# A gate and up product of seven half products with running sums in PSUM, and the quantizer of h behind attention's sums, in a linear-attention layer gated by an FP4 feed-forward net

## Chip, cores and metric

One core of one Trainium2 chip runs one program. The engines are PE (TensorE, the matmuls), DVE (VectorE), ACT (ScalarE), POOL (GpSimd) and SP (SyncE, which here only issues DMAs). The metric is the device time of one execution in microseconds (us); lower is better. Everything is float32 unless a type is named.

## What is computed

For an input x of 4 x 2048 tokens by 256 features:

```python
xn = layernorm(x)
# attention and its own feed-forward net
Q, K = elu(xn @ Wq + bq) + 1, elu(xn @ Wk + bk) + 1      # 16 heads of 64
V    = xn @ Wv + bv
KV   = einsum("bshd,bshm->bhdm", K, V)                    # sums over all 2048 tokens of a batch
Z    = 1 / (einsum("bshd,bhd->bsh", Q, K.sum(axis=1)) + EPS)
o    = einsum("bshd,bhdm,bsh->bshm", Q, KV, Z)
x1   = layernorm(xn + o @ Wo + bo) * g1 + be1
s    = layernorm(x1 + gelu(x1 @ W1 + b1) @ W2 + b2) * g2 + be2
# the gate: a feed-forward net whose inputs and weights are rounded to FP4 in blocks of 16
h    = silu(fp4(xn) @ fp4(w_gate).T) * (fp4(xn) @ fp4(w_up).T)   # 704 wide
g    = silu(fp4(h) @ fp4(w_down).T)
out  = x + s * g
```

`fp4(t)` divides each block of 16 neighbours by the block's largest absolute value over 6, rounds to the eight magnitudes 0, 0.5, 1, 1.5, 2, 3, 4, 6, and multiplies the scale back in.

## The kernel before

The 8192 tokens are cut into 32 blocks of 256 tokens (T), eight to a batch; a block is two tiles of 128 tokens (j = 0, 1). KV needs all keys of a batch before its first query, so the keys of batch 0 are made in a start phase (lines 1055 to 1152), and the keys of batch b+1 are made beside the queries of batch b. A pass over keys handles one half (f) of the key features for one block of tokens, two such passes to each query block: f=0 for the first four blocks of a batch, f=1 for the other four. The f=0 keys are normalized from x in the stage ahead, stored, and transposed by DMA (`keys_apart`: ACT copies into a tile with the tag "e", which the e of Q uses too); the f=1 keys are loaded again. Blocks 24 to 31 have no keys beside them. The keys of a stage are made ready in the stage before.

The loop over n (line 1170 on) is a pipeline. Stage n finishes block n's quantized h and x in qT, makes `sums` of its queries (pz, then z = 1/pz on DVE, stored to DRAM as z_d and read back as zb, each row spread over 64 partitions), runs `gate_up(n+1)`, `down(n)`, multiplies Q by zb (`qz`), runs `attention(n)` with its normalization, the second half of the feed-forward net of block n-1 (py), its output, the queries of block n+1 (pq) and the first half of the feed-forward net of block n (pf). On PE each stage is therefore: pk, pz, pxk, pg, pd, pk, pa, pxk, py, pt_x, pscale, py, pq, pf.

What sets the order. `mm` (line 102) and `tr` (105) keep PE's instructions in program order. DVE and ACT go through the `Ordered` helper (111 to 122, so all their rows show L119): in program order in the start phase, and from line 1145 on in an order that the scheduler chooses ahead of time, within waits that `tc.issue_after` adds. Every DMA of the stages is issued from SP's queue, one after the other, and an issue that waits holds up those behind it. All matmuls share four PSUM banks of the tag "mm" and some accumulators.

Around the gate: `gate_up` (753) makes, for each token tile j and each half i of 352 columns, a gate product and an up product in one bank each, over two 128-deep chunks c of the features: 16 matmul calls. ACT takes silu of the one bank, DVE multiplies by the other. The weights are `wgu`, [128, chunk, gate columns then up columns], filled in `quantize_gu` from transpositions. After the third product pair the instruction named "late" ends; `qz` waits for it.

The quantizer of h has two parts: `scales_h` (701; a reduction of 704 columns, the scale, its reciprocal) and `grid_of_h` (704; h times reciprocal, ACT's `m_h`, rounding onto h, and the grid in bfloat16), for each j. The grid is transposed by DMA into gridT (738); the scales of h and x go through PE (`pscale`), ACT, a DRAM tile scale_d (726) and eight spreading DMAs (729) into qT, and `quantized_x` and `quantized_h` (742, 748) multiply the two.

Attention in the first three batches is a product by seven as well (`seven_sums`, `seven_products`, `add_seven`, lines 889 to 922): `attention_sums` makes four sums of halves of Q (zs) behind qz. `WEIGHT` (880) names which weight each of the seven products takes. `m_of_half` (608) turns the key sums pxk into the matrix of a half of the heads when its last keys are done; it reloads wv (616), copies pxk to xk, stores a row of it (631) and reads that back as kh (636).

Of the kernel before, what the change touches and what calls it, by code (L numbers as in the profile page):

```python
# [8 lines left out]
F32 = mybir.dt.float32  # L9
# [13 lines left out]
def linear_attention_gated_by_fp4_ffn(  # L23
# [228 lines left out]
    wv_sb, wv_d = {}, {}  # L252

    def load_wv(f, dep):
        wv_sb[f] = batch.tile([P, ND, HALF], F32, tag="wv", name=f"wv_{f}", bufs=1)
        load_when(dep, wv_sb[f], by_chunks(Wv)[:, :, f * HALF : (f + 1) * HALF])

    def wv_bias(f):
        bias_in_row0("v", wv_sb[f], f, nc.gpsimd)
        wv_d[f] = dram.tile([P, ND, HALF], F32, tag=f"wv_d{f}", name=f"wv_d{f}", bufs=1)  # L260
        nc.sync.dma_start(wv_d[f], wv_sb[f])
        if f > 0:
            del wv_sb[f]

    cols = {}

# [69 lines left out]
        return x.rearrange("p (k e) -> p k e", e=BLK)  # L336


    wgu = const.tile([P, ND, 2 * I], F32, name="wgu")
    wd = const.tile([P, NI, D], F32, name="wd")  # L340
    nc.gpsimd.memset(wd[TAIL:, NI - 1, :], 0.0)

# [28 lines left out]
    def quantize_gu(ks):  # L371


        w = work.tile([P, I], F32, tag="h", name=f"wgu_{ks[0]}")
        for i, k in enumerate(ks):
            lo, hi = k * P, (k + 1) * P
            cs = slice(i * D, (i + 1) * D)
            if hi <= I:
                nc.sync.dma_start(w[:, cs], w_gate[lo:hi, :])
            elif lo >= I:  # L380
                nc.sync.dma_start(w[:, cs], w_up[lo - I : hi - I, :])
            else:
                nc.sync.dma_start(w[: I - lo, cs], w_gate[lo:I, :])
                nc.sync.dma_start(w[I - lo :, cs], w_up[: hi - I, :])
        yield from quantize_weight(w, len(ks) * D, f"wgu_{ks[0]}")
        for i, k in enumerate(ks):
            pt = mm_tile(f"pwgu_{k}")
            for c in range(ND):
                lo = i * D + c * P
                tr(pt[:, c * P : (c + 1) * P], w[:, lo : lo + P], ident)  # L390
            scalar.copy(
                wgu[:, :, k * P : (k + 1) * P], pt[:, : ND * P].rearrange("p (c k) -> p c k", c=ND)
            )
        yield

    def load_down():
# [211 lines left out]
    def m_of_half(b, f, dep=None, ahead=False):  # L608


        nm = f"{b}_{f}"
        if wv_sb.get(f) is not None:
            wv = wv_sb.pop(f)
        else:
            wv = batch.tile([P, ND, HALF], F32, tag="wv", name=f"wv_{nm}", bufs=1)
            nc.sync.dma_start(wv, wv_d[f])
        wo = batch.tile([P, 4, D], F32, tag="wo", name=f"wo_{nm}", bufs=1)
        load_when(dep, wo, by_chunks(Wo)[:, 4 * f : 4 * f + 4, :])
        if ahead:
# [3 lines left out]
            nc.gpsimd.memset(kh[b], 0.0)  # L623
        m = m_sb[b, f] = batch.tile([P, 4, D], F32, tag=f"m{f}", name=f"m_{nm}", bufs=2 - f)
        pxk = keys.pop((b, "pxk", f))
        xk = batch.tile([P, ND, HALF], F32, tag="xk", name=f"xk_{nm}", bufs=1)
        for d in range(ND):
            scalar.copy(xk[:, d, :], pxk[d])

# [112 lines left out]
    def quantized_x(n):  # L742

        qx = qT[:, NI:, :]
        t = gridT[n][:, NI * TB :, :].rearrange("p (c j) t -> p c (j t)", j=TB)
        return vector.tensor_tensor(qx, qx, t, ALU.mult)

    def quantized_h(n, j):

# [1 line left out]
        return vector.tensor_tensor(qh, qh, gridT[n][:, j * NI : (j + 1) * NI, :], ALU.mult)  # L751

    def gate_up(n):
        blk[n]["h"] = []
        for j in range(TB):
            h = work.tile([P, I], F32, tag="h", name=f"h_{n}_{j}")
            blk[n]["h"].append(h)
            for i in range(2):
                halves = []
                for part in range(2):  # L760
                    pg = mm_tile(f"pg_{n}_{j}_{i}_{part}")[:, :IH]
                    lo = part * I + i * IH
                    for c in range(ND):
                        mm(
                            pg, qT[:, NI + c, j * P : (j + 1) * P], wgu[:, c, lo : lo + IH],
                            start=c == 0, stop=c == ND - 1,
                        )
                    halves.append(pg)
                    if part == 0:
                        yield  # L770
                hh = h[:, i * IH : (i + 1) * IH]
                scalar.activation(hh, halves[0], AF.Silu)
                ins = vector.tensor_tensor(hh, hh, halves[1], ALU.mult)
                if (j, i) == (1, 0):
                    blk[n]["late"] = ins.ins
                yield

    def down(n, j):
        if j == 0:
# [285 lines left out]
    for n in range(NB):  # L1065
# [50 lines left out]
        if n == 5:  # L1116
            add_b2(dep)
        if n == 6:
            load_xn(0)
            scales_x(0)  # L1120
            spread_scales(-1, False, True)
# [6 lines left out]
    load_xn(1)  # L1128
    load_xnT(0)

    step(gate, 4)
    step(ready)
    step(m_0)
    scales_h(0, 0)
    scales_x(1)
    step(gate, 4)
    scales_h(0, 1)
    step(m_0, 2)
    m_half = m_of_half(0, 1)
# [30 lines left out]
    for n in range(NBLK):  # L1170
# [78 lines left out]
            load_xn(n + 2)  # L1249
        if subs:  # L1250
            keys_xk(b + 1, subs[1])
            if subs[1] % NB == NB - 1:
                m_half = m_of_half(b + 1, subs[1] // NB)
                step(m_half)
        bn, bin_ = divmod(n + 1, NB)
        next_subs = (2 * bin_, 2 * bin_ + 1) if bn + 1 < B else ()
        for sub in next_subs if n > 0 else ():
# [2 lines left out]
            ffn_2(n - 1, 20)  # L1260
        more = n + 1 < NBLK, n + 2 < NBLK
        if more[0]:
            scales_h(n + 1, 0)
            behind = zs_ins if n == 0 else None if subs else qz_ins
            with tc.issue_after(behind) if behind is not None else nullcontext():
                scales_h(n + 1, 1)
            if more[1]:
                scales_x(n + 2)
        for sub in next_subs if n == 0 else ():
# [13 lines left out]
            spread_scales(n + 1, *more)  # L1283
        if n > 0:
            ffn_2(n - 1, 28)
        if more[0]:
            q_of(n + 1)
        if n == 0:
# [73 lines left out]
```

## Time and profile before

| what | value |
| --- | --- |
| median of 3 runs | 1878.16 us (1877.71 to 1878.72) |
| span of the profiled execution | 1880.7 us |
| one stage with keys (18, first pg to the next first pg) | 1248.93 - 1192.49 = 56.44 us |
| one stage of the last batch (28) | 1756.63 - 1712.49 = 44.14 us |
| first pg of the start phase | 127.91 us |

The profile is of one execution and its times stand against its own span. In a row of the groups the columns are line, engine, operation, out<-in with partitions x elements and type, count; then busy time, mean ns of one; then the engine's idle time just before such rows and what ended most of it. In a timeline a row is start, duration, engine, line, operation, tiles, count, and in brackets the idle time before it with what ended it. A matmul of float32 shows as two instructions. Durations of neighbours overlap a little, as the engines are pipelined, so steps are also taken from start to start.

### The profile page before, as it was taken

The numbers are of one execution on the slowest core, as the hardware profiler recorded it, in microseconds if no ns is written. First come the engines' busy times: TensorE is split into PE (matmuls) and PEld (weight loads), VectorE is DVE, ScalarE is ACT, GpSimd is POOL, SyncE is SP. The second block draws the span as 40 slices with busy tenths as digits, with TensorE's granted clock in tenths as the row PEclk, the third lists the DMA queues.
The fourth block names the chain that finished last, engine by engine and source line by source line (L and its number), as shares of the span: only waits on it lengthen the run. The fifth ranks groups of instructions, "written<-read, shape, count | busy, mean of one in ns | idle before, by whom it ended". The sixth has DMA issues, their size and how long they took to land.

```text
span 1880.7 us, 25219 instructions
## 1 busy us (share of the span) xinstructions
PE 1861.7 (99%) x9324; PEld 1383.0 (74%) x9324; DVE 1363.6 (73%) x2526; ACT 706.7 (38%) x1191; POOL 386.9 (21%) x371
## 2 busy tenths in 40 slices
PE   9999999999999999999999999999999999999998
PEld 4456677777777777777677787777777788888887
DVE  5676777766677877777667787776676767777775
ACT  2333544333334335443233533353322333333332
POOL 1411322011122212220112221122101122222212
PEclk9999999999999999999999999999999999999999
DMA  5526564434535456635344544564543544444442
GB/s 184 193 73 130 117 124 103 96 101 94 96 64 94 115 98 122 143 66 111 80 89 79 117 100 103 96 139 87 95 86 72 104 75 87 82 90 83 88 84 54
DMA packets 229434, 188.78 MB, mean 100 GB/s; under 512 B 107687, under 2 KB 191155, under 8 KB 229310
## 3 DMA queue, kind: packets, MB, share of 16 engines
q1 hardware_dynamic: 228476, 185.58, 47.4%
q8 instruction: 74, 1.21, 0.3%
q10 hardware_dynamic: 834, 1.58, 0.3%
q14 instruction: 50, 0.41, 0.1%
HBM read 131.96 MB, written 32.59 MB: 87 GB/s over the span
## 4 chain that ended last, share of the span: by engine, by line
PE 78%; DVE 11%; DMA 7%; issue 1%; POOL 1%; SPq 1%; ACT 1%; POOLq 0%; ACTq 0%; DVEq 0%
PE pg L103 13%; PE pf L103 11%; PE pk L103 10%; PE pxk L103 10%; PE pq L103 9%; PE pa L103 8%; PE pd L103 7%; PE py L103 7%; DMA zb<-z_d 3%; PE pz L103 2%; DMA z_d<-z 1%; DVE y L119 1%; DMA xn<-xn_d 1%; DVE x L119 1%; DVE hs L119 1%
## 5 line engine op out<-in xcount | busy, mean ns | idle before, releaser
L430 POOL TENSOR_TENSOR rstd<-rstd,neg_half 128x2 f32<-128x2 f32 (+1 forms) x98 | 77.8, 795 | 1298.0 <-DVE rstd L119 984.9
L103 PE MATMUL pg<-wgu,qT 128*128 128x352 f32 x1024 | 308.5, 459 | 0.1
L103 PEld LDWEIGHTS pg<-wgu,qT 128*128 128x128 f32 x1024 | 194.3, 190 | 113.7 <-issue 11.5
L103 PE MATMUL pk<-wk_sb,xnT_k 128*128 128x512 f32 x512 | 230.4, 592 | 1.2 <-ACT xnT_k L119 1.2
L103 PE MATMUL pq<-xnT,wq_sb 128*128 128x256 f32 x1024 | 227.6, 380 | 1.5 <-DVE zq L119 1.4
L103 PE MATMUL pxk<-kk,xn_k 128*128 128x512 f32 x496 | 227.9, 598 | 1.0 <-DVE kk L119 1.0
L103 PE MATMUL pf<-x1T,w_sb 128*128 128x256 f32 x1024 | 227.2, 380 | 1.1 <-DVE zq L119 0.6
L103 PEld LDWEIGHTS pf<-x1T,w_sb 128*128 128x128 f32 x1024 | 193.8, 190 | 30.4 <-DVE zq L119 4.0
L103 PEld LDWEIGHTS pq<-xnT,wq_sb 128*128 128x128 f32 x1024 | 191.8, 190 | 27.7 <-DVE zq L119 3.1
L119 DVE SCALAR_TENSOR_TENSOR kk<-ek,pk 128x512 f32<-128x512 f32 x128 | 85.6, 685 | 173.2 <-ACT ek L119 173.2
L103 PE MATMUL pd<-wd,qT 128*128 128x256 f32 x768 | 172.9, 380 | 0.0
L103 PEld LDWEIGHTS pk<-wk_sb,xnT_k 128*128 128x128 f32 x512 | 97.0, 190 | 102.6 <-issue 89.0
L119 ACT ACT_TABLE_LOAD x121 | 155.2, 1283 | 40.9 <-PE pk L103 26.0
L119 ACT ACTIVATE x1T<-pt_x,bcol 128x256 f32<-128x256 f32 x64 | 32.7, 561 | 359.3 <-PE pt_x L106 359.3
L103 PEld LDWEIGHTS pd<-wd,qT 128*128 128x128 f32 x768 | 145.3, 190 | 26.4 <-issue 2.5
L103 PEld LDWEIGHTS pxk<-kk,xn_k 128*128 128x128 f32 x496 | 89.4, 190 | 99.1 <-issue 87.3
L119 DVE TENSOR_TENSOR h<-h,pg 128x352 f32<-128x352 f32 x128 | 66.1, 517 | 107.1 <-PE pg L103 104.0
L119 ACT ACTIVATE h<-pg 128x352 f32<-128x352 f32 x128 | 58.9, 460 | 209.8 <-PE pg L103 209.7
L119 ACT ACTIVATE hT<-pf,bcol 128x256 f32<-128x256 f32 x256 | 106.1, 472 | 66.7 <-PE pf L103 66.3
L119 DVE TENSOR_TENSOR zq<-zq,zb 128x1024 f32<-128x1024 f32 x64 | 78.9, 1232 | 68.9 <-DMA zb<-z_d 68.8
L103 PE MATMUL py<-w_sb,hs 128*128 128x128 f32 x992 | 122.0, 275 | 0.0
L119 ACT ACTIVATE e<-pq,neg_one 128x512 f32<-128x512 f32 x128 | 86.2, 685 | 83.7 <-PE pq L103 71.2
(161 smaller groups left out, 2777.8 us busy)
## 6 DMA issues: line engine op xcount, KB each, us to landing
zb<-z_d SPq DMA_DIRECT2D x128, 256.0 KB, 6.2
qT<-scale_d SPq DMA_DIRECT2D x248, 128.0 KB, 6.0
x_k<-in_L_attn_src_dram SPq DMA_DIRECT2D x32, 256.0 KB, 4.1
x<-in_L_attn_src_dram SPq DMA_DIRECT2D x32, 256.0 KB, 2.9
xn_d<-xn_k SPq DMA_DIRECT2D x32, 256.0 KB, 2.5
xn<-xn_d SPq DMA_DIRECT2D x32, 256.0 KB, 2.7
xnT_d<-xnT_k SPq DMA_DIRECT2D x32, 256.0 KB, 2.0
xnT<-xnT_d SPq DMA_DIRECT2D x32, 256.0 KB, 4.3
```

The source lines that it names most:

```text
L103: return tc.keep_in_program_order(nc.tensor.matmul(*args, **kw))
L119: ins = op(*args, **kw)
L430: pool["last"] = nc.gpsimd.tensor_tensor(rstd[:, j0:j1], rstd[:, j0:j1], neg_half[:, j0:j1], ALU.pow).ins
```

## The change

Five edits go together.

1. `gate_up` splits the product into halves three ways: two token tiles, two feature chunks, and gate or up columns. Seven products of halves replace eight (the scheme that attention uses), each for two column halves u: 14 matmul calls. The weights are seven [128, 704] tiles, of which four are sums that POOL makes once, in the start phase. The left sides need four 128 x 128 sums of quantized x, which DVE makes behind `quantized_x`. The products are not summed by VectorE alone: a product is accumulated onto a bank that already holds others, after ACT or DVE has read the sum so far.
2. The quantizer's scales of h (both j) come behind the instruction `zs_ins`, or `qz_ins` in the last batch, in every stage.
3. To make room, wv and xk share a tile with the tag of zb, the first loads of wv use the tag of wo, and wv is reloaded from DRAM each time.
4. `m_of_half` of the loop starts behind the last part of `ffn_2(n - 1)`.
5. The end of the start phase is ordered anew: the weight of `down` first, then the gate, with the scales of h behind its parts.

```diff
+    wgu = const.tile([P, 7, I], F32, name="wgu")
+    def gate_sums():
+        nc.gpsimd.tensor_tensor(wg("t3"), wg("22"), wg("t1"), ALU.subtract)
+        nc.gpsimd.tensor_tensor(wg("t1"), wg("t1"), wg("11"), ALU.subtract)
+        nc.gpsimd.tensor_tensor(wg("t2"), wg("22"), wg("t1"), ALU.subtract)
+        nc.gpsimd.tensor_tensor(wg("t4"), wg("21"), wg("t2"), ALU.subtract)
...
+        t = work.tile([P, 2, ND, HALF], F32, tag="zb", name=f"wv_xk_{nm}", bufs=1)
+        wv, xk = t[:, 0], t[:, 1]
+        nc.sync.dma_start(wv, wv_d[f])
...
     def quantized_x(n):
-        return vector.tensor_tensor(qx, qx, t, ALU.mult)
+        vector.tensor_tensor(qx, qx, t, ALU.mult)
+        s = blk[n + 1]["xs"] = work.tile([P, 4, P], F32, tag="x1T", name=f"xs_{n + 1}", bufs=1)
+        h = quarters_of(qx)
+        vector.tensor_tensor(s[:, 0], h["21"], h["22"], ALU.add)
+        vector.tensor_tensor(s[:, 1], s[:, 0], h["11"], ALU.subtract)
+        ins = vector.tensor_tensor(s[:, 3], h["12"], s[:, 1], ALU.subtract)
+        vector.tensor_tensor(s[:, 2], h["11"], h["21"], ALU.subtract)
+        return ins
...
     def gate_up(n):
+        run = banks("pg")
+        product(1, run, True)
+        for u in range(2):
+            scalar.copy(h[0][:, part[u]], run[u])
+        yield
+        other = banks("pg5")
+        product(5, other, True)
+        for u in range(2):
+            scalar.copy(up[1][u], other[u])
+        yield
+        product(6, run, False)
+        for u in range(2):
+            scalar.copy(up[0][u], run[u])
+        yield
+        product(3, other, False)
+        for u in range(2):
+            vector.tensor_tensor(up[0][u], up[0][u], other[u], ALU.add)
+        yield
+        product(7, run, False)
+        for u in range(2):
+            vector.tensor_tensor(up[1][u], up[1][u], run[u], ALU.add)
+        yield
+        last_ = banks("pg2")
+        product(2, last_, True)
+        for u in range(2):
+            hh = h[0][:, part[u]]
+            vector.tensor_tensor(hh, hh, last_[u], ALU.add)
+            scalar.activation(hh, hh, AF.Silu)
+            blk[n]["late"] = vector.tensor_tensor(hh, hh, up[0][u], ALU.mult).ins
+        yield
+        product(4, run, False)
+        for u in range(2):
+            hh = h[1][:, part[u]]
+            scalar.activation(hh, run[u], AF.Silu)
+            vector.tensor_tensor(hh, hh, up[1][u], ALU.mult)
+        yield
...
+            gate_sums()
             load_xn(0)
...
+    step(ready)
     step(gate, 4)
-    step(ready)
     step(m_0)
+    scales_x(1)
+    step(gate, 2)
     scales_h(0, 0)
-    scales_x(1)
-    step(gate, 4)
+    step(gate, 1)
     scales_h(0, 1)
...
-            scales_h(n + 1, 0)
-            behind = zs_ins if n == 0 else None if subs else qz_ins
-            with tc.issue_after(behind) if behind is not None else nullcontext():
-                scales_h(n + 1, 1)
+            with tc.issue_after(zs_ins if in_seven(b) else qz_ins):
+                for j in range(TB):
+                    scales_h(n + 1, j)
...
             ffn_2(n - 1, 28)
+        if subs and subs[1] % NB == NB - 1:
+            m_half = m_of_half(b + 1, subs[1] // NB)
+            step(m_half)
```

`product(i, bank, start)` makes product i for both column halves; `start=False` accumulates onto what the bank holds.

## Prediction

> **What bounds the kernel now.** I read the page's engine totals and clock first, then the chain that ended last, then the groups by shape, and then timelines of one block of each kind.
>
> ```profile
> PE 1861.7 (99%) x9324; PEld 1383.0 (74%) x9324; DVE 1363.6 (73%) x2526; ACT 706.7 (38%) x1191; POOL 386.9 (21%) x371
> ...
> PEclk9999999999999999999999999999999999999999
> ...
> PE 78%; DVE 11%; DMA 7%; issue 1%; POOL 1%; SPq 1%; ACT 1%; POOLq 0%; ACTq 0%; DVEq 0%
> ...
> L103 PE MATMUL pg<-wgu,qT 128*128 128x352 f32 x1024 | 308.5, 459 | 0.1
> ...
> L119 DVE TENSOR_TENSOR zq<-zq,zb 128x1024 f32<-128x1024 f32 x64 | 78.9, 1232 | 68.9 <-DMA zb<-z_d 68.8
> ```
>
> TensorE is busy 99% of the span at an even clock, so a matmul left out should be time left out. But a fifth of the chain is VectorE, DMA and POOL: in places TensorE is only just fed. The last row says where: VectorE idles 68.8 us for zb, the row of 1/z spread over partitions through DRAM.
>
> Blocks with f=0 keys (n = 1, 2, 7-10, 15-18), f=1 keys (4-6, 12-14, 20-22) and the last batch (24-30) differ. I take one of each; a time with a plus is in microseconds from the first pg (the gate product) of its block, which starts at 904.70 in n=13, 1192.49 in n=18, 1712.49 in n=28. Block 13, TensorE then VectorE:
>
> ```profile
> 904.70 9.63 PE L103 MATMUL pg<-wgu,qT 128*128 128x352 f32 x32
> 914.16 5.34 PE L103 MATMUL pd<-wd,qT 128*128 128x256 f32 x24
> ...
> 926.10 2.05 PE L103 MATMUL pa<-m,zs 128*128 128x128 f32 x16 [0.48 <-DVE zs L119]
> ...
> 937.97 0.87 PE L106 MATMUL pt_x<-ident,x 128*128 128x128 f32 x4
> ```
>
> ```profile
> 918.07 1.23 DVE L119 TENSOR_TENSOR zq<-zq,zb 128x1024 f32<-128x1024 f32 x1 [4.88 <-DMA zb<-z_d]
> ...
> 937.50 0.73 DVE L119 TENSOR_SCALAR x<-x,mv,rstd 128x256 f32<-128x256 f32 x2 [0.82 <-POOL rstd L430]
> ```
>
> The transposition pt_x starts 0.47 after the second normalization row: there VectorE sets the time. Its chain starts at zb, at +13.37. Block 18, TensorE, ACT, VectorE:
>
> ```profile
> 1227.05 7.07 PE L103 MATMUL pq<-xnT,wq_sb 128*128 128x256 f32 x32
> 1233.96 7.07 PE L103 MATMUL pf<-x1T,w_sb 128*128 128x256 f32 x32
> ```
>
> ```profile
> 1230.30 0.68 ACT L119 ACTIVATE e<-pq,neg_one 128x512 f32<-128x512 f32 x1
> ```
>
> ```profile
> 1231.33 0.68 DVE L119 SCALAR_TENSOR_TENSOR zq<-e,pq 128x512 f32<-128x512 f32 x1
> ```
>
> Here pt_x is early enough, but pq's four banks are emptied by e (ACT) and zq (VectorE), and the first e comes 1.5 us after its bank is full, behind the key copies. The spare time is small.
>
> **The product.** pg occupies 914.16-904.70 = 9.46 us for eight products' worth, 1.18 each. Seven take 8.28. Before the product needed 16 calls, now 14; the gain per block is 1.18, and over 32 products 37.9 us if TensorE alone set the time. Inside the gate each running sum is read by ACT (copy of 352 columns, 0.46 by the h<-pg row) or VectorE (0.52 by its h row) before the next product goes onto the bank; the next product on that bank comes one whole other product (1.18) later, so two reads (about 0.95) just fit. I take no stall; were 0.2 lost at each of the four reuses, 0.8 of the 1.18 would go. VectorE's ten small operations (four before) end with h's last multiplication at about +9.8; before, qz could start at +8.65 where zb was there.
>
> **Sums of quantized x.** Four 128x128 operations on VectorE ahead of z: 128x512 takes 0.69, 128x256 0.42, so I take 0.24 each, 0.9 together. In f=1 blocks z_d's DMA waits in SP's queue anyway (issued at +1.57, z done at -0.3): hidden. In f=0 blocks z_d was issued at -0.3, so zb comes 0.9 later, +9.95 in place of +9.05, as late as h is done (+9.8). In the last batch VectorE idled 1.20 for pz: hidden when the four take 0.9. But POOL's addends run there then. In block 28 VectorE's y took 1.44 and 1.72 beside a POOL row of 1.85; elsewhere y takes 0.69 and that POOL row 1.27. So up to 1.1 late, bound by one POOL operation; I take 0.3 x 7 = 2.
>
> The Trainium skill has a rule on this ("SBUF — State Buffer", section "SBUF: two separate sides"): VectorE with two SBUF inputs and a GpSimd operation that reads SBUF take turns at one port pair, each for a whole instruction. By it the sums in the last batch would wait a whole POOL operation of 1.27, and the seven blocks lose some 7 us instead of my 2. The stretched y rows speak for it.
>
> **The quantizer of h** goes behind the sums. In f=1 blocks I added VectorE's start-to-start steps in the order of the changed program, from the first qz to pt_x: qz 2.3, zs 2.4, two reductions 1.6, scales 0.2, kk 1.2, hs 2.5, reciprocals 0.7, two scalings of h 1.6, x additions 2.2, reduction of xn 0.6, rounding of h 0.8, statistics 1.2, grid 0.8, POOL's rstd and normalization 1.4: 19.4. Before it was 19.9 (n=13) to 20.7 (n=4): one more reduction and scaling (2.0), but h's second half (0.4), y (0.6, now inside POOL's time) and a wait for xn (0.9; its load no longer stands behind gridT in SP's queue) are gone. So pt_x comes 0.5 to 1.3 earlier, where TensorE could use 1.18: n=5, 6, 13, 14, 21, 22 give 4.3 together. In n=4, 12, 20 zb came late (+13.3 to +14.8). SP's queue in block 12:
>
> ```profile
> 847.80 0.42 SPq L616 DMA_DIRECT2D wv<-wv_d  x1
> 848.32 0.38 SPq L854 DMA_DIRECT2D z_d<-z  x1
> 853.66 2.57 SPq L859 DMA_DIRECT2D zb<-z_d  x4
> ```
>
> z_d stands behind 512 KB of wv and lands 5.3 after its issue (3.2 to 4.6 in the other f=1 blocks). The change loads wv two stages earlier, so I take a gain of 2 each, between 0.7 (the chain alone) and 3.9 (all that pt_x was late): 6. Sum 10.3. The moved m_of_half also puts kh's two DMAs behind out; the next z could wait 0.4 in three blocks, nothing taken.
>
> **f=0 blocks.** Here all of the quantizer now stands between zs and the key normalizations, and the time that VectorE had free for half of it during the gate is not used. By the same steps: zs ends at +14.6; reductions and scales to +16.4; kk waits for its ek until +17.4; kk 1.2, hs 2.4, x and two scalings of h to +26.3; rounding and statistics to +29.2; three times POOL's rstd (0.9 with its way) with a grid (0.8) between, and the second normalization of keys ends at +33.95. Before it was 1225.64 + 0.74, +33.9: VectorE gained nothing. From there y 0.6, s 0.6, h 0.8, y 0.6, grid 0.8 and 0.7, s 0.45 bring the first zq to +38.5, done at +39.1 (before 1231.33 + 0.68, +39.5). ACT's m_x, two pairs of copies (1.1 each) and e end at +38.0, in time for that. TensorE, 1.18 early, has pq at 1227.05 - 1192.49 - 1.18 = +33.4, its fourth bank, a quarter of 6.91 each, due at +38.6 and pf at +40.3. The second e waits until the first copies (+36.3) are transposed, 3.45 by block 18's rows: +39.75, its zq done at +41.0, which frees pf's first bank. So pf starts at +41.0 to +41.45; before 1233.96, +41.47. The 1.18 is eaten: gain 0 to 0.45, I take 0.2 x 10 = 2. Were it 0.5 worse each, 5 lost.
>
> **Last batch.** In the normalization's path stand rounding (0.80), grid (0.80) and s (0.60): pt_x at +24.0 against TensorE's +22.25 (before +23.43). The gap before pscale (0.2) and that before pf (0.26) go instead, pf starts at +33.3 (before +33.34): gain 0, less the 2 above.
>
> **Free blocks** (3, 11, 19, 23) keep 1.18: 4.7. Block 0 had gaps; 1.5.
>
> **Start.** Four POOL operations of 128x704 stand ahead of POOL's rstd of the last keys. POOL's 128x512 rows take 1.27 to 2.13; so 1.75 to 2.9 each, 7 to 11.6 us from 109.6, after the last copy of wgu. VectorE in order waits with kk, which started at 117.27; TensorE's pxk (118.67) then starts 2 to 7 later. I take 4.7, less the 1.18 of the first product: 3.5 lost. Cover that is certain (an earlier rstd) would make it -1.
>
> **Sum.** 10.3 + 4.7 + 1.5 + 2 - 2 - 3.5 = 13.0 us. The profiled execution's span is 1880.7; 1880.7 - 13.0 = 1867.7. The median of the runs is 1878.2, 2.5 less than that span: 1865.
>
> **Rivals.**
> *A, TensorE sets the time everywhere* (VectorE's and ACT's chains catch up by using their idle times, 27% and 62%): 1880.7 - 37.9 = 1842.8, or 1847.5 with the stall at the start; less 2.5: 1840 to 1845. For it: the 99%. Against it: +39.1 against +38.6, and pt_x 0.47 behind VectorE. 15%, with all up to 1856.
> *B, the new chains eat all*: the start loses 6, the last batch 0.4 x 7 = 2.8, the three wv blocks and the f=0 blocks gain nothing: 4.7 + 1.5 + 4.3 - 6 - 2.8 = 1.7 gained, 1880.7 - 1.7 - 2.5 = 1876.5. For it: in seventeen of the 31 blocks my steps leave next to nothing already. Against it: wv's reload does leave the queue ahead of z_d. 15%.
> *C, slower: the four sums ahead of z take twice their time* (as the y rows did beside POOL), 2.0 for 0.9. qz in f=0 blocks then starts at +11.05, 1.1 later than h allows, and the tail with it; in the last batch zb's second half comes 1.1 later. 17 x 1.1 = 18.7 lost against 10.3 + 4.7 + 1.5 - 3.5 = 13.0: 1880.7 + 5.7 - 2.5 = 1884. It decides from 13.0 / 17 = 0.76 per block on, sums of about 1.7. Against it: in f=0 blocks POOL ends its last addition 2.2 before z starts. 15%, with other losses on VectorE's path.
> That the change doesn't do what it says: ACT or VectorE cannot empty a running sum in time and the gate still takes 9.5; then the 4.7 goes, and 1.18 of block 0: 1865 + 5.9 = 1871, within the forecast's range.
>
> **Chances.** Forecast (1856 to 1874.4): 55%; A 15%, B 15%, C 15%. The measurement can tell about 0.2% from no change, 1874.4 to 1881.9. Faster: 55 + 15 = 70%; same 15%; slower 15%. The range 1845 to 1882 leaves out C (15%) and the lower end of A (about 5%).
>
> **What would show it.** pg of 8.3 us per block with 28 rows, no gap in it; pt_x in f=1 blocks waiting on VectorE still, at +31 to +33; in f=0 blocks a gap of 0.5 to 1 before the last pq or pf, released by zq; in the last batch a gap of about 1.7 before pt_x; a gap of 2 to 7 before pxk near 118. No gaps in the f=0 blocks would mean A; zb later than +10.5 there, C.

## The result and the profile after

The changed kernel takes 1936.29 us (median; 1927.75 to 1940.44), the kernel before 1878.26 on the same chip: a ratio of 1.0307 with an interval of 1.0281 to 1.0332. The forecast was 1865. The profiled execution of the changed kernel has a span of 1926.0 (own time 1927.75) at a mean granted clock of 0.995; the other three executions have 0.989 to 0.991 and take 7 to 13 more. So this trace explains 45.3 us of the loss (1926.0 - 1880.7). The rest fits the lower clock of the other executions: 0.004 to 0.006 of 1936 us is an estimated 8 to 12 us. More on the clock below.

The page after: engine totals, clock, shares of the chain that ended last, and the two kinds of gate matmul.

```profile
PE 1841.7 (96%) x9196; PEld 1367.1 (71%) x9196; DVE 1499.2 (78%) x2846; ACT 792.6 (41%) x1384; POOL 400.0 (21%) x375
...
PE 43%; DVE 30%; DMA 17%; SPq 3%; issue 2%; POOL 2%; ACT 2%; DVEq 0%; POOLq 0%; ACTq 0%
...
L103 PE MATMUL pg<-wgu,xs 128*128 128x352 f32 x512 | 157.5, 460 | 2.1 <-DVE z L119 2.1
...
L103 PE MATMUL pg<-wgu,qT 128*128 128x352 f32 x384 | 124.7, 461 | 2.0 <-DVE up L119 1.8
```

The product did what it says. The gate's matmuls went from 308.5 us to 272.0 (the two rows add up to more, as their neighbours overlap), and one gate takes 8.45 in place of 9.63, with waits inside it of 1.3 and 2.5 in the first two blocks (n = 0 and 1) and of 0.2 in one more (n = 27). But TensorE fell from 99% to 96% of a longer span, and its part of the chain from 78% to 43%: VectorE (30%) and the transfers that it sets off (17%) have taken over. VectorE is busy for 135.6 us more, 4.2 per block; part of this is rows stretched beside GpSimd. Added up over the trace, TensorE now waits 34.5 us at pt_x for the normalized x (1.1 before) and 17.1 us at pq for zq (1.4 before).

To see where, I took each stage's length, first pg to the next first pg, minus that of the same stage before, and added by kind. "Start" is the time to the first pg with the first stage, "edge" is n = 1 and the blocks where batches meet, n = 7, 8, 15, 16, and "f=0" is the other blocks of that kind; "wv" is n = 4, 12, 20. Plus is lost; each row is one profiled execution against that of the kernel before. The last column counts stretches of 3.41 us in which the granted clock was 0.50, those of the last 15 us left out; each costs at most 1.7 us.

| run | start | n=0 | f=1 | wv | free | f=0 | edge | n=24 | 25 to 30 | sum | clock falls |
| --- | --- | --- | --- | --- | --- | --- | --- | --- | --- | --- | --- |
| predicted | 3.5 | -1.5 | -4.3 | -6 | -4.7 | -1 | -1 | 0.3 | 1.7 | -13 |  |
| after | 5.2 | 0.2 | 0.8 | -3.8 | 6.8 | 0.9 | 15.8 | -1.5 | 21.0 | 45.3 | 6 |
| 1 sums behind z | 5.3 | 1.1 | 8.7 | -2.5 | -2.0 | 3.2 | 18.2 | -1.5 | 9.3 | 39.8 | 9 |
| 2 addends behind sums | 6.3 | 1.6 | 2.2 | -3.8 | 5.8 | 1.4 | 19.5 | -1.5 | 14.4 | 45.7 | 11 |
| 3 quantizer as before | 5.6 | -0.7 | 3.5 | -3.6 | 4.6 | 3.6 | 14.2 | -1.5 | 23.0 | 48.7 | 7 |
| 4 quantizer alone | -0.1 | 0.5 | 10.0 | 6.5 | 0.7 | -1.4 | 2.7 | 0.0 | 7.7 | 26.5 | 4 |
| 5 xk in its own tile | 5.3 | -1.4 | 1.6 | -3.3 | 3.6 | 2.0 | 14.0 | -0.1 | 19.2 | 41.0 | 5 |
| 6 h behind norm | 4.8 | -1.3 | -7.9 | -5.0 | -1.0 | 1.9 | 18.2 | 2.0 | 16.6 | 28.5 | 5 |
| 7 = 1 and 5 | 5.5 | 0.0 | 6.0 | -4.1 | -2.5 | 0.8 | 12.6 | -1.5 | 11.0 | 27.9 | 7 |
| 8 = 1, 5 and 6 | 4.8 | 2.9 | -5.5 | -5.1 | -3.8 | -0.7 | 7.7 | 1.0 | 5.3 | 6.6 | 4 |
| 10 = 8 and three orders | 2.5 | 1.0 | -6.3 | -3.3 | -4.6 | -0.6 | 7.3 | 0.2 | 1.6 | -2.2 | 0 |
| 11 addends left out | 5.1 | -1.0 | 2.8 | -3.2 | 7.6 | 1.3 | 19.0 | -1.3 | 1.4 | 31.7 | 5 |
| 12 = 10 and two orders | 2.1 | 0.0 | -6.9 | -5.0 | -4.7 | -1.0 | 10.9 | 0.1 | 5.0 | 0.3 | 2 |

(The predicted 2 for the f=0 blocks is split over their two columns, and that of the last batch by its blocks. The kernel before has no clock fall.) Run 9 has no row, as its profiled execution ran at a granted clock of 0.933 throughout (1980.26 us), and that execution is left out of its times too. As falls come in some executions and not in others, a difference of 2 us or so in one column is no result by itself. Two columns hold 36.8 of the 45.3: the last batch and the edges.

**The last batch.** Block 28 of the changed kernel, VectorE and then GpSimd from the multiplication of x on; GpSimd's three rows, which prepare the addends of the gate's output, are called addends below (start, duration, engine, line, operation; a row of x2 holds two):

```profile
1742.36 0.69 DVE L119 TENSOR_TENSOR qT<-qT,gridT 128x512 f32<-128x512 f32 x1
1743.15 1.51 DVE L119 TENSOR_TENSOR xs<-qT 128x128 f32<-128x128 f32 x2
1744.59 1.35 DVE L119 TENSOR_TENSOR xs<-xs,qT 128x128 f32<-128x128 f32 x1
1745.98 1.24 DVE L119 TENSOR_TENSOR xs<-qT,xs 128x128 f32<-128x128 f32 x1
1747.14 0.41 DVE L119 TENSOR_SCALAR z<-pz 128x256 f32<-128x256 f32 x1
```

```profile
1743.05 1.26 POOL L863 TENSOR_TENSOR o<-g,be_r 128x512 f32<-128x512 f32 x1
1744.39 1.40 POOL L864 TENSOR_TENSOR o<-o,x 128x512 f32<-128x512 f32 x1
1745.76 1.31 POOL L865 TENSOR_TENSOR g<-g,g_r 128x512 f32<-128x512 f32 x1
```

Each of VectorE's three rows of xs ends just behind a GpSimd row: 1744.66, 1745.94 and 1747.22 against 1744.31, 1745.79 and 1747.07. Four sums for which I had taken 0.9 last 4.0 (1743.15 to 1747.14); in blocks 24 to 30 it is 3.0 to 4.1. (Block 24 loses nothing by it: its zb comes at +9.8 all the same.) z, due right behind them, starts 0.65 after the gate's first matmul (1746.49). In block 28 of the kernel before it started 2.56 ahead of it (1712.49), and pt_x waited for nothing:

```profile
1709.93 0.42 DVE L119 TENSOR_SCALAR z<-pz 128x256 f32<-128x256 f32 x1 [1.20 <-PE pz L103]
```

```profile
1735.92 0.68 PE L106 MATMUL pt_x<-ident,x 128*128 128x128 f32 x4
```

Downstream on TensorE, after the change:

```profile
1759.22 7.38 PE L103 MATMUL pa<-m,zq 128*128 128x256 f32 x32 [0.80 <-DVE zq L119]
...
1772.66 0.87 PE L106 MATMUL pt_x<-ident,x 128*128 128x128 f32 x4 [2.48 <-DVE x L119]
```

The bracket is TensorE's idle time and its releaser: attention waits 0.8 for zq, and pt_x 2.48 for the normalized x. pt_x starts at +26.2, predicted was +24.0. The wait of pt_x is 2.48 or 2.49 in each of the blocks 25 to 30.

**The start.** GpSimd's rows after, and the wait on TensorE that answers to them:

```profile
109.36 1.76 POOL L344 TENSOR_TENSOR wgu<-wgu 128x704 f32<-128x704 f32 x1 [7.55 <-ACT wgu L119]
111.20 2.19 POOL L345 TENSOR_TENSOR wgu<-wgu 128x704 f32<-128x704 f32 x1
113.47 2.20 POOL L346 TENSOR_TENSOR wgu<-wgu 128x704 f32<-128x704 f32 x1
115.75 1.67 POOL L347 TENSOR_TENSOR wgu<-wgu 128x704 f32<-128x704 f32 x1
117.38 1.14 POOL L445 TENSOR_TENSOR rstd<-rstd,neg_half 128x2 f32<-128x2 f32 x1
```

```profile
115.93 0.30 PE L106 MATMUL pscale_-1_833<-ident,scale 128*128 128x128 f32 x1 [3.18 <-DVE scale L119]
116.06 7.01 PE L103 MATMUL pk<-wk_sb,xnT_k 128*128 128x512 f32 x12
```

The same two rows before:

```profile
113.38 0.30 PE L106 MATMUL pscale_-1_828<-ident,scale 128*128 128x128 f32 x1 [0.39 <-DVE scale L119]
113.52 5.32 PE L103 MATMUL pk<-wk_sb,xnT_k 128*128 128x512 f32 x12
```

rstd comes behind the four sums, at 117.38 (113.18 before), and the first gate starts at 133.15, 5.2 later. But the longest wait is not for rstd: VectorE's scale of x, which needs nothing from GpSimd, is late as well, since rows ahead of it are stretched (the last scaling of w_down 2.24 for 0.89, a two-element rstd row 1.03 for 0.16). So pscale is 2.55 late; behind that wait the clock is 0.50 for 3.41 us, and pk takes 1.69 longer. pxk then starts at 122.91, 4.24 later than before (118.67). VectorE's kk, which stands behind the wait for rstd, ends at 122.86, so pxk could not have started sooner at a full clock either.

**The f=1 chain.** Block 13 on VectorE, from qz, and the transposition that ends the chain on TensorE:

```profile
936.74 1.23 DVE L119 TENSOR_TENSOR zq<-zq,zb 128x1024 f32<-128x1024 f32 x1 [2.49 <-DMA zb<-z_d]
938.58 1.23 DVE L119 TENSOR_TENSOR zq<-zq,zb 128x1024 f32<-128x1024 f32 x1 [0.62 <-DMA zb<-z_d]
...
956.88 0.73 DVE L119 TENSOR_SCALAR x<-x,mv,rstd 128x256 f32<-128x256 f32 x2 [0.59 <-POOL rstd L445]
```

```profile
957.35 0.87 PE L106 MATMUL pt_x<-ident,x 128*128 128x128 f32 x4 [1.67 <-DVE x L119]
```

957.35 - 936.74 = 20.6, where 19.4 was predicted and 19.9 measured before. In the six plain f=1 blocks the chain takes 20.6 to 21.5, and 19.9 to 20.6 before. Its start (zb) came earlier in five of the six, by 1.1 in block 13 (+12.27 for +13.38), which pays for most of it.

**Free blocks** (n = 3, 11, 19, 23). SyncE's queue in block 19 (here the number behind the start is what the issue took), and the issue of z_d before:

```profile
1273.02 0.32 SPq L515 DMA_DIRECT2D xn_k<-xn_d  x1
1273.43 0.39 SPq L516 DMA_DIRECT2D xnT_k<-xnT_d  x1
1273.91 0.38 SPq L848 DMA_DIRECT2D x<-in_L_attn_src_dram  x1
1274.38 0.38 SPq L909 DMA_DIRECT2D z_d<-z  x1
1278.32 1.91 SPq L914 DMA_DIRECT2D zb<-z_d  x3
```

```profile
1249.54 0.38 SPq L854 DMA_DIRECT2D z_d<-z  x1
```

z is 1.0 later, so the issue of z_d, at +0.6 and behind one load before, now falls behind three loads, at +1.56. z_d takes 3.9 to land behind them, zb comes at +13.0 in place of +10.0, and pt_x waits 2.8. In the four free blocks, for which I predicted the full 1.18 each, pt_x waits 2.30, 1.50, 2.80 and 0.07, and they lose 6.8; in the last of them, n = 23, it is the next block's pz that waits, 1.33 for kh (run 5).

**The clock.** In block 19 the granted clock falls after that wait. Windows (us, then busy time and count of PE, PEld, DVE, ACT, POOL, then PEclk, DMA share, GB/s):

```profile
1304.00:1306.80 2.80, 0.04 (x1) 0.00 (x0) 2.21 (x8) 0.00 (x0) 1.07 (x1) 1.00 0.17 33
1306.80:1308.80 2.00, 1.97 (x12) 1.78 (x13) 1.45 (x3) 1.06 (x4) 0.00 (x0) 0.75 0.28 52
1308.80:1311.00 2.20, 2.20 (x12) 2.20 (x12) 0.00 (x0) 0.99 (x4) 0.00 (x0) 0.50 0.13 35
1311.00:1313.00 2.00, 2.00 (x10) 1.78 (x10) 1.83 (x4) 1.60 (x3) 0.00 (x0) 0.95 0.38 84
```

After 2.8 us without matmuls the next 4 us run at 0.75 and 0.50, and the 16 py matmuls there take 3.48 in place of 1.95. So a wait of 2.8 cost about 4.3. The wait of 2.48 in block 28 was followed by no fall, and one of 2.48 in block 25 was (0.50 for 2 us): whether a fall follows is not given by the length alone.

The trace has the granted clock of every moment. In this execution it falls to 0.50 six times before the end, each time for 3.41 us, starting at 116.55, 676.34, 1307.80, 1628.65, 1819.80 and 1867.59, at or behind waits of 2.48 to 3.18. Counted from the first, these starts are 164, 349, 443, 499 and 513 times 3.4133 us away, and in the other profiled runs with more than one fall they lie on such a grid too. So within an execution falls begin only at such fixed moments, and where a wait lies between two of them may decide, not only its length. What decides the runs do not show: in run 2 a wait of 1.68 was followed by a fall, and in run 1 one of 3.44 (at the start) by none. Six falls are at most 10.2 of the 45.3 us, up to 5.1 of them in the last batch (n = 25, 29, 30).

### The profile page after: what moved, and what is told of

Read it like the earlier page. It is cut to its first block, busy times and chain, and to the rows that moved or that the text cites. A ratio compares the mean times of both kernels' runs of the same rounds, so it can differ in the third digit from the quotient of the medians.

```text
span 1926.0 us, 25477 instructions
## 1 busy us (share of the span) xinstructions
PE 1841.7 (96%) x9196; PEld 1367.1 (71%) x9196; DVE 1499.2 (78%) x2846; ACT 792.6 (41%) x1384; POOL 400.0 (21%) x375
## 4 chain that ended last, share of the span: by engine, by line
PE 43%; DVE 30%; DMA 17%; SPq 3%; issue 2%; POOL 2%; ACT 2%; DVEq 0%; POOLq 0%; ACTq 0%
DMA zb<-z_d 8%; PE pf L103 8%; PE pk L103 7%; PE pq L103 7%; PE pxk L103 6%; PE pg L103 4%; PE py L103 3%; DVE h L119 3%; DVE x L119 3%; DVE hs L119 3%; DVE scale L119 3%; DMA z_d<-z 3%; DVE zq L119 3%; PE pd L103 2%; DMA gridT<-grid 2%
## 5 line engine op out<-in xcount | busy, mean ns | idle before, releaser
L445 POOL TENSOR_TENSOR rstd<-rstd,neg_half 128x2 f32<-128x2 f32 (+1 forms) x98 | 82.0, 837 | 1322.5 <-DVE rstd L119 997.5
L103 PE MATMUL pq<-xnT,wq_sb 128*128 128x256 f32 x1024 | 230.8, 382 | 17.1 <-DVE zq L119 17.1
L119 ACT ACT_TABLE_LOAD x121 | 155.2, 1283 | 36.8 <-PE pk L103 21.5
L103 PE MATMUL pg<-wgu,xs 128*128 128x352 f32 x512 | 157.5, 460 | 2.1 <-DVE z L119 2.1
L103 PEld LDWEIGHTS pg<-wgu,xs 128*128 128x128 f32 x512 | 97.2, 190 | 57.2 <-DVE z L119 3.8
L119 ACT ACTIVATE m_h<-h 128x704 bf16<-128x704 f32 x64 | 50.9, 795 | 194.6 <-DVE h L119 194.6
L103 PE MATMUL pg<-wgu,qT 128*128 128x352 f32 x384 | 124.7, 461 | 2.0 <-DVE up L119 1.8
L103 PE MATMUL py<-w_sb,hs 128*128 128x128 f32 x992 | 126.6, 282 | 0.0
```

Of the source, the lines that this page charges most:

```text
L103: return tc.keep_in_program_order(nc.tensor.matmul(*args, **kw))
L119: ins = op(*args, **kw)
L445: pool["last"] = nc.gpsimd.tensor_tensor(rstd[:, j0:j1], rstd[:, j0:j1], neg_half[:, j0:j1], ALU.pow).ins
```

## The experiments

My theory was that the added VectorE work costs by its place (beside GpSimd's rows, ahead of z, between qz and pt_x) and not by its amount; the rival, that VectorE simply has too much work now.

**1. The sums of x behind z.** The four sums move out of `quantized_x` and are issued behind z's reciprocal.

```diff
-        vector.tensor_tensor(qx, qx, t, ALU.mult)
+        return vector.tensor_tensor(qx, qx, t, ALU.mult)
+
+    def x_sums(n):
+        qx = qT[:, NI:, :]
...
             ins = sums(n, ins.ins)
+            with tc.issue_after(ins.ins):
+                x_sums(n)
```

> The changed kernel with the four sums of quantized x behind z's reciprocal instead of ahead of it. Theory A (the sums ahead of z are the main loss: 0.9 us of VectorE on the way to zb, and up to 4.2 us where they meet POOL's additions in the last batch): z, z_d and zb come 0.9 to 3.3 us earlier, the last batch gets back 12 to 18 of the 21 us that it lost, blocks 1, 3, 11 and 19 some 6 more: 1905 to 1915 us against 1936. Theory B (the quantizer behind the sums of Q lengthens VectorE's chain to the normalization, and that is the main loss): zb earlier helps little, 1930 to 1936.

Measured: 1918.74 (1917.01 to 1922.25), ratio 1.0223 (1.0208 to 1.0238): between the two ranges. The last batch regains 11.7 of 21.0, and the free blocks go from 6.8 lost to 2.0 gained. The f=1 blocks lose 7.9 more. Three clock falls lie in them (in n = 13, 14 and 21), up to 5.1 of it; the rest I did not find: in block 13 z_d leaves the queue at +1.56 as in the changed kernel, but takes 4.5 to land in place of 3.9, and pt_x waits 2.64.

**2. GpSimd's addends behind the sums.** In the last batch `gpsimd_behind` waits for the sum that the program writes last, in place of the first half of quantized h.

```diff
-            gpsimd_behind(qT[:, 0, :])
+            gpsimd_behind(blk[n + 1]["xs"][:, 2, :])
```

> The changed kernel, but in the last batch POOL's additions (gate and feed-forward addends) start only when the last of the four sums of quantized x is written. Theory A (the collision of these sums with POOL's additions): the four sums take 0.9 to 1.2 us again where they took 4.2, pt_x of the last batch comes 2 to 3 us earlier per block, in all 12 to 18 us: 1918 to 1924. Theory B (the quantizer): no more than 3 us, 1933 to 1939.

Measured: 1927.38 (1923.60 to 1928.28), ratio 1.0263 (1.0248 to 1.0278): between the two ranges. The last batch regains 6.7 of 21.0, less than taking the sums away from z. The edit freed only part of the sums: in block 28 the scheduler places the sum that GpSimd waits for among the first two, so the fourth still meets the first addend (1.37 for 0.29), and the four take 2.11, not the 0.9 to 1.2 that I expected.

**3. The quantizer as before**, edit 2 undone in the changed kernel.

```diff
-            with tc.issue_after(zs_ins if in_seven(b) else qz_ins):
-                for j in range(TB):
-                    scales_h(n + 1, j)
+            scales_h(n + 1, 0)
+            behind = zs_ins if n == 0 else None if subs else qz_ins
+            with tc.issue_after(behind) if behind is not None else nullcontext():
+                scales_h(n + 1, 1)
```

> The changed kernel with edit 2 undone: the scales of h are ordered as in the kernel before. Theory A: the waits of pt_x in blocks with f=1 keys and in the last batch shrink by about 1 us each, 5 to 15 us in all, since VectorE can use its waits for zb: 1921 to 1931. Theory B: most of the loss goes, 1885 to 1900.

Measured: 1930.30 (1928.37 to 1935.90), ratio 1.0287 (1.0266 to 1.0309): in theory A's range. By the medians it is 6 less than the changed kernel, but the executions of the two overlap, and the profiled one is 3.3 longer.

**4. The quantizer alone**, the same edit made in the kernel before.

> The kernel before with edit 2 alone: the scales of h (both tiles) behind the sums of Q. Theory A: VectorE's chain from qz grows by one reduction and one scaling (2.0 us) less what leaves it; TensorE waits at pt_x in the last batch and in the f=1 blocks by 0.5 to 1 us, 1883 to 1895 against 1878. Theory B: 1905 to 1930.

Measured: 1913.79 (1908.95 to 1914.25), ratio 1.0188 (1.0173 to 1.0204): 36 lost, in theory B's range and above theory A's (1883 to 1895). The f=1 and wv blocks lose 16.4, at pt_x; block 13's chain takes 21.4. Runs 3 and 4 belong together. Alone, edit 2 costs 36; undone beside the product, it gives back 6 at most. My reading, which no run tests by itself: before, h is half done in the middle of the gate, and its quantizer can lie beside the matmuls; the new product finishes both tiles of h only with its last two products, so that cover is gone whether the scales are held back or not.

**5. xk in a tile of its own**, and `m_of_half` at its old place: edits 3 and 4 undone as far as the space allows (for b > 0).

```diff
+            wv = work.tile([P, ND, HALF], F32, tag="zb", name=f"wv_{nm}", bufs=1)
+            xk = work.tile([P, ND, HALF], F32, tag="zs", name=f"xk_{nm}", bufs=1)
```

> The changed kernel with edits 3 and 4 partly undone: in the loop xk has a tile of its own (with the tag of zs, free at that time) in place of one shared with wv, zb and the sums of the feed-forward net, and m_of_half starts where it did before. Theory A (the shared tile makes the copy of the key sums wait for the last py, so kh lands after pz wants it): pz of blocks 8, 16 and 24 waits no longer (1.3 to 2.0 us each), and blocks 7, 8, 15 and 16 get back most of the 11 us that they lost: 1922 to 1929 us against 1936. Rival (these edits cost nothing of note): 1933 to 1939.

Measured: 1929.15 (1923.46 to 1931.81), ratio 1.0274 (1.0257 to 1.0291), at the edge of theory A's range. It addresses this wait of the changed kernel (block 8; 1.99 and 1.33 in blocks 16 and 24):

```profile
626.55 0.64 PE L103 MATMUL pz<-zq,kh 128*32 128x256 f32 x8 [1.56 <-DMA kh<-k_d]
```

kh, the sum of keys, is stored and read back only after xk was copied, and xk's copy waited for the tile that it shares with zb and hs, until the last py. In this run pz waits for kh nowhere. Alone this is worth 7 by the medians and 4 by the profiled executions.

**6. h's scaling behind the normalization.** VectorE's first step of `grid_of_h` (h times reciprocal, both j) is held back until attention's normalization is issued.

```diff
-            grid_of_h(n + 1, 0)
+            normal = blk[n]["normal"]
+            grid_of_h(n + 1, 0, None, normal)
```

> The changed kernel with the scaling of h by its reciprocals (and with it the rounding) issued behind attention's normalization, so that it does not stand in the way from zb to pt_x. Theory A (VectorE's chain from zb to the normalization sets pt_x in f=1 blocks and in the last batch): these chains get 2.4 to 4 us shorter, the waits of pt_x (0.9 to 2.6 us) go, and with them the clock's falls behind waits of 2.5: 1905 to 1920. Rival (VectorE is full, so what is moved behind the normalization is late for zq, and TensorE waits at pq or pf instead): 1930 to 1945, with gaps before pq and pf in f=0 blocks of 2 us and more.

Measured: 1919.22 (1910.94 to 1922.09), ratio 1.0209 (1.0182 to 1.0237). That is in theory A's range. The f=1 blocks turn from +0.8 to -7.9, more than I had predicted for them at the outset, and their chain takes 18.9 to 19.6; the free blocks go from 6.8 to -1.0. n = 7 and 15 lose 2.9 and 3.4 more: kh is later still, and pz of the blocks behind them waits 4.8 and 5.9 for it.

**7 and 8. The orders together**: 1 with 5, then 1 with 5 and 6.

> Sums of quantized x behind z, and xk in a tile of its own with m_of_half as before. If the two losses are separate the gains add, 18 + 9: 1905 to 1914 us. If both run into the same full VectorE, less than 22 of 27: above 1914.

> Sums of quantized x behind z, xk in a tile of its own, and the scaling of h behind the normalization. Theory A (these three chains are the loss, the seven products themselves gain): 1870 to 1895 us, pt_x without waits, f=0 blocks near 56.4. Rival (VectorE's 136 us of added work are the loss, wherever they stand): 1905 or more.

Measured: 7 takes 1911.07 (1908.96 to 1912.69), ratio 1.0173 (1.0157 to 1.0188); 8 takes 1889.02 (1887.13 to 1890.53), ratio 1.0055 (1.0040 to 1.0070), in theory A's range. Run 7 gives 25 of the 27, so these two losses are separate. Run 8 settles the rival. VectorE has the same 2846 instructions and is busy for 1497.3 us, against 1499.2 in the changed kernel, and 47 of the 58 us are back. In block 13 pt_x waits for nothing (no bracket):

```profile
943.88 0.87 PE L106 MATMUL pt_x<-ident,x 128*128 128x128 f32 x4
```

The last batch has a new wait, as h's two scalings now stand ahead of the scale of x, which GpSimd's addends stretch:

```profile
1743.14 0.33 PE L106 MATMUL pscale<-ident,scale 128*128 128x128 f32 x1 [1.98 <-DVE scale L119]
```

**9. The kernel before with the edit of run 6.**

> The kernel before with one edit, that of the run with h behind the normalization: VectorE's scaling of h (1.6 us for both tiles) is held back until attention's normalization is issued. It asks whether what that order gained in the changed kernel is a gain of its own. Theory: it is not. In the kernel before, h is ready half a gate earlier and its scaling lies beside the gate's matmuls, where nothing waits for VectorE; held back, it stands between the normalization and the elu of zq, as in the block n = 7 of the earlier run (+5 there): the blocks of n = 0, 7, 8, 15, 16 lose 1 to 3 each, those of the last batch 1 to 2 (h's scaling ahead of the scale of x), the rest gains or loses under 1, so 1885 to 1900, slower than the 1878 of before. Rival (the order is better whatever the product): the 1 to 2 that the f = 1 blocks gained there come here too, 1860 to 1872, and then the comparison of the combined version with the kernel before would flatter it.

Measured: 1901.32 (1900.41 to 1901.36), ratio 1.0127 (1.0112 to 1.0143): 24 slower, just above theory's range. The order that helps the changed kernel hurts the kernel before, so run 8 is not flattered by a gain of its own.

**10. Three orders more.** GpSimd's sums of weights behind the first kk of the last key tile; in the last batch h behind the scale of x; h left free in n = 0, 7, 15, 23.

```diff
+            gpsimd_behind(dep)
+            with tc.issue_after(pool["last"]):
+                gate_sums()
...
+            normal = None if n == 0 or (subs and bi == NB - 1) else blk[n]["normal"]
+            if not subs and more[1]:
+                normal = scaled[f"x_{n + 2}"]
```

> The combined version (sums of x behind z, xk in a tile of its own, h behind the normalization) with three more orders, each for a place where its trace still loses to the kernel before: GpSimd's four sums of the gate's weights come behind the first kk of the last key tile in place of ahead of that stage's rstd (start, +4.8 there); in the last batch h's scaling comes behind the scale of x, so that pscale does not wait (1.98 in five blocks); in n = 0 and in the last block of a batch h's scaling is left free (+2.9 and +2.6). The same work on every engine. Theory (the loss is the place of the added VectorE and GpSimd work, not its amount): start -2 to -3, n = 0 -3, n = 7 -1, n = 24 to 29 -10, so 1889 - 17 = 1872, between 1868 and 1880. Rival (VectorE with its 1497 us of work is now the bound, and a wait that is removed comes back elsewhere in the same block): 1885 to 1892. For the start alone: if the gate's first product begins within 1 us of the kernel before's 127.9, GpSimd's queue was the cause there; if it stays 3 or more late, it is the sums' collision with VectorE's rows.

Measured: 1882.13 (1878.28 to 1891.52, 11 runs), ratio 1.0028 (1.0016 to 1.0040). 7 of the expected 17 came, which is between the two ranges. The last batch gave 4.5 of 10, for quantized h now comes late there, and pd waits 0.55 for it in four of the blocks, 1.21 and 1.56 in two more. At the start the first gate begins 2.8 late, between my two marks. pxk is on time again (118.61), so the 4.24 that it was late came from the sums at their old place, by rstd's queue and by the stretched rows; the two are not told apart. What is left came with the sums to new rows (a scaling of w_down takes 1.96 for 0.89, the multiplication of x 1.57 for 0.69), and with the transposes of w_down, which the change puts ahead of the gate:

```profile
129.98 0.87 PE L106 MATMUL pwd<-ident,w_down 128*128 128x128 f32 x6 [1.97 <-DVE w_down L119]
```

Its profiled execution is 2.2 shorter than that of the kernel before, but the medians say 0.28% longer, and they decide.

**11. The addends left out.** In n = 24 to 30 GpSimd's three addends of g and o are dropped and x stands in for o; the sums stay where the change has them.

```diff
+        o = x if left_out(n) else work.tile([P, TB, D], F32, tag="o", name=f"o_{n}")
...
     def gate_addend(n):
+        if left_out(n):
+            return
```

> The changed kernel with GpSimd's three addends of the gate's output (o and g, 1.26 to 1.4 us each) left out in the blocks n = 24 to 30: the x tile takes the place of o, so the last batch's rows are not the reference's. Nothing is moved on VectorE: the sums of x stay ahead of z. It prices the collision by itself. Theory (each of VectorE's short sums waits for a whole GpSimd row): in n = 25 to 30 the four sums fall from 4.2 to about 0.9 us, z lands some 3 earlier, the wait of pt_x falls from 2.5 to at most 1.2, and of the 21 us that these blocks lost 12 to 20 come back: 1916 to 1925. Rival (the sums cost by their place ahead of z, whatever GpSimd does): under 5 come back, 1931 to 1936.

Measured: 1917.18 (1914.18 to 1917.89), ratio 1.0212 (1.0196 to 1.0228), in theory's range. VectorE in block 28, and pt_x:

```profile
1739.28 0.49 DVE L119 TENSOR_TENSOR xs<-qT 128x128 f32<-128x128 f32 x2
1739.69 0.28 DVE L119 TENSOR_TENSOR xs<-xs,qT 128x128 f32<-128x128 f32 x1
1740.01 0.29 DVE L119 TENSOR_TENSOR xs<-qT,xs 128x128 f32<-128x128 f32 x1
```

```profile
1766.60 0.87 PE L106 MATMUL pt_x<-ident,x 128*128 128x128 f32 x4 [1.50 <-DVE x L119]
```

The sums take 0.94 (1739.28 to 1740.22, where z starts), pt_x waits 1.5 at +23.9, and blocks 25 to 30 lose 1.4 together: 19.6 of 21.0 us go with the addends. 16 of that is the time that the sums themselves were stretched in the six blocks, and no clock fall is left there. The kernel before was not run without its addends, so what they cost it is not taken off. What is left is what I had predicted for the last batch without a collision: +24.0, a gap of about 1.7, nothing gained.

**12. Two orders on top of run 10**: GpSimd's addends behind the sums in n = 1 and the last batch; the gate's first product ahead of the last transposes of w_down.

```diff
-    step(ready)
-    step(gate, 4)
+    step(gate, 1)
+    step(ready)
+    step(gate, 3)
```

> The run with four more orders, and two on top: GpSimd's addends come behind the sums of x in n = 1 and in the last batch, so the sums no longer meet them; and the gate's first product, which needs none of the weights' sums, goes ahead of the last transposes of w_down, which waited 1.97 for VectorE. The same work. Theory: start -0.8 to -1.2, n = 1 -1.5 to -2.2 (its pg waits of 0.41 and 1.79 go), last batch -2 to -4, so 1882 - 5 = 1877, between 1874 and 1880: level with the kernel before within 0.2%. Rival: the addends, now later, meet the adds of the gate's results and the second half of h, and take back what the sums gain: 1881 to 1886.

Measured: 1887.20 (1882.85 to 1888.53), ratio 1.0044 (1.0032 to 1.0057): the rival's range. The first gate starts at 127.89, as early as before the change, and then waits inside for VectorE and ACT, so the start keeps 2.1 of its loss; block 1 and the last batch lose more than in run 10; in the last batch one of the four sums still meets an addend (1.36). No order that I tried beats the kernel before.

## Why the prediction was wrong

It said 1865, and the time was 71 more. The sum gained 13.0 where the profiled execution lost 45.3. By its own steps:

- **The product**: right. 1.18 per gate, 28 rows in 8.45, and 8.28 from the first start to the next product's, as worked out; no stall from the reuse of the banks.
- **Sums of x, last batch: the step that failed most.** "I take 0.3 x 7 = 2", with a bound of one GpSimd operation. The four sums took 4.0 in place of 0.9, since not one but three of them in succession were held to the end of a GpSimd row. I had the sign of it in the stretched y rows (1.44 beside a row of 1.27, 1.72 beside the one of 1.85) and the count wrong: four short operations in a row meet three GpSimd rows, a single long one meets one. Without the addends 19.6 us came back (run 11). The Trainium skill's rule that I set aside ("SBUF — State Buffer", section "SBUF: two separate sides") has the two engines take turns for whole instructions, and the ends of the rows of block 28 agree with that within 0.35 us. My reading of it, one operation of 1.27 per block and some 7 in all (seven times 1.27 is 8.9), was too small too.
- **Sums of x, elsewhere**: "hidden" was right in f=1 blocks, where z_d leaves the queue at +1.56 as before, but the free blocks were taken to "keep 1.18" without a look at what SyncE's queue issues in the 1.0 by which z is later there. Three loads come ahead of z_d, one before, and these blocks lose 6.8 in all. Run 1 turned that into 2.0 gained.
- **The f=1 chain**: predicted 19.4, measured 20.6. Mis-sized were the first terms: qz 3.1 for 2.3 (zb's second half lands later, a wait of 0.62), and zs 2.7 for 2.4; from hs to pt_x the sum holds (11.8 measured, 11.8 predicted). 1.2 a block is as much as pt_x was to come earlier, so the six plain blocks lose 0.8 in place of gaining 4.3. That VectorE's rows between qz and pt_x decide here, run 6 shows. The wv blocks kept 3.8 of the 6: wv leaves z_d's way as predicted (in block 12 its load is issued 24 us ahead of z_d, though one stage early and not two). In blocks 4 and 20 pt_x no longer waits and TensorE sets what they gain, 1.2 and 2.5; in block 12 pt_x waits 0.85 for the longer chain, and 0.1 is gained.
- **The quantizer of h**: I counted what it costs at its new place, and took the place itself as free in f=1 since the chain still came out shorter. Run 4 shows that it costs 36 without the product. The prediction weighed both edits only in sum, and so never asked whether they use up the same cover.
- **f=0 blocks**: right where they are plain. I predicted a gap of 0.5 to 1 released by zq and pf at +41.0 to +41.5; block 18 has 1.06 and +41.65, and the five lose 0.9. Wrong at the edges, for which I used the same steps: pq waits there for zq 2.2, 1.5, 2.6 and 2.1 (n = 1, 7, 8, 15). In block 1 the sums also meet GpSimd (3.9 for 0.9; pg waits 1.7 and 0.8), kh is late by 1.56, 1.99 and 1.33 in blocks 8, 16 and 24, where I had written 0.4 and "nothing taken", and behind the wait in block 8 the clock falls. No single order cured the edges; 8 together halved them. Which of the added rows holds up zq there is left open.
- **Start**: predicted 3.5 lost, measured 5.2. The four sums took 7.8 and pxk starts 4.24 later, both near the terms of the sum (7 to 11.6, 4.7). But the 1.18 of the first product did not come off: in the first stage pscale waits 1.55 for the scale of h (0 before), which was not in the sum.
- **The clock**: I treated it as even. After waits of 2.48 to 3.18 it fell to 0.50 for 3.41 us, six times, at most 10.2 us of the profiled execution; in block 19 that adds 1.5 to a wait of 2.8. The changed kernel's median lies 8.5 above that execution. The Trainium skill ("TensorE: Matmul & The Clock Gate", section "Part 1: The HAM clock gate") speaks of idle windows of about 3.4 us that halve the clock; here waits of 2.48 were enough in three blocks, and the depth, 0.50, agrees.

Of the rivals, C named the mechanism (the sums beside GpSimd) and set its price at 1.1 per block in 17 blocks. It is real in six blocks of the last batch, at 3.3 each, and does not touch the plain f=0 blocks, where the sums take 0.9 and zb comes at +9.7 (C's sign was later than +10.5); I had spread it over ten f=0 blocks and seven of the last batch. A fell: TensorE waits 51.6 us at pt_x and pq for VectorE. B had the new chains eat the gain; they cost more than the gain.

## What to carry to other kernels

When work leaves the busiest engine and returns as many short operations on another, price each of them against what runs beside it: count how many rows of the engine that it takes turns with (here GpSimd) a chain of short operations meets, not how much time it has. Before taking a delay as hidden, list what other queues issue within it. And when two edits use the same idle time as cover, weigh each alone as well as both: undoing one shows little as long as the other stays.

## What the runs showed of the hardware

VectorE's two-input sums of 128x128, 0.29 each when alone, ended 0.15 to 0.35 behind GpSimd's rows of 1.26 to 1.40 when these ran beside them, three times in succession. GpSimd's own rows were stretched less: 128x704 took 1.67 to 2.20, 128x512 1.25 to 2.31. The granted clock fell to 0.50 for 3.41 us at a time, behind waits of TensorE as short as 1.68 (run 2) but not behind one of 3.44 (run 1), and within one execution all falls started whole multiples of 3.4133 us apart.
